# Splitting VectorE's tasks into single instructions, and a planner that ranks by remaining work

## The chip, the core and the metric

The kernel runs on one core of a Trainium2 chip. The metric is the device time of one execution in microseconds (us), the median of several runs. The core has a matrix engine (TensorE; PE in the profile, PEld for its weight loads), a vector engine (VectorE, DVE), a scalar engine (ScalarE, ACT), a general engine (GpSimd, POOL) and queues for transfers (here those of SyncE, SP). Each works through its own list of instructions in the order in which the program issued them; an instruction that needs something of another engine waits, and what is behind it in the list waits too.

## What is computed

Two transformer layers over 16 sequences of 256 tokens with 128 features, all in float32. Each of the four sublayers is added to its input and normalized:

```python
x = L0_attn_hidden_states
x = _layernorm(x + attention0(x))          # 16 heads of 64, softmax over 256 keys
x = _layernorm(x + routed_spline_ffn(x))   # argmax over 8 clusters, then 8 tiles; table lookup
x = _layernorm(x + gated_attention1(x))    # linear attention, and a window of 65 keys, 16 heads of 8
x = _layernorm(x + moe_block(x))           # causal attention, 16 heads of 64, l2-normed q and k;
                                           # then 8 experts 128-512-128
```

The last block is itself two parts: causal attention with a layer norm, and eight experts that all run on all tokens, `gelu(h @ w1[e] + b1[e]) @ w2[e] + b2[e]`, summed with softmax gates and normalized again.

## The kernel before

The 4096 tokens are cut into eight groups of 512 tokens (`NG`, two sequences each), and each group passes five stages: `stage_a` (first attention), `stage_b` (spline feed-forward), `stage_c` (linear and window attention), `stage_d` (causal attention and gates), `stage_e` (the experts). The intermediate results stay on the chip. Buffers are slots of classes (`SLOTS`, lines 39 to 63): five slots for a group's tokens (`x`), five for the experts' hidden values (`hid`), one for their sum (`e`), four PSUM banks (`p`, 512 values of float32 per partition each) and two double banks for scores (`s`).

No loop sets the order of the instructions. Each stage hands tasks to a planner, `Plan.add(eng, cost, fn, r, w, ...)` (line 101): an engine letter (P TensorE, V VectorE, S ScalarE, G GpSimd, Q the queue of transfers; two letters leave the choice to the planner), an estimated cost in ns, a function that issues the instructions, and the objects read and written. An object may be given with a part, `(object, part)`; accesses with different parts don't order each other (line 117). What a task needs but only to hold a slot is given as `hold`. Each task carries a place `at`, which is the group's number plus the stage's offset (`OFF`, 0 to 4) plus a fraction inside the stage.

`Plan.order` (line 144) then simulates all engines. At each step it takes, for each engine, the ready task with the smallest key and among these the smallest again:

```python
key = (start, at, t.seq)
```

`start` is the earliest moment by the planner's own clock: the engine free, each predecessor's end plus a lag (`LAG` by the predecessor's engine, or `OWN` on the same engine), a slot free. A table load of ScalarE adds `SWITCH`, a change of TensorE's tiling mode adds `DRAIN`. So `at` decides only between tasks with equal start. While ScalarE is in a `burst` (the gelus of two experts, eight tasks) it takes nothing else. The instructions are issued in the order of the list that results; the framework adds the waits that the data need. Objects such as `chain_a`, `chain_c`, `chain_d`, `chain_e` are written by the tasks of one kind so that these keep their order.

Tasks of several VectorE instructions in the kernel before: `layernorm` (statistics, line 530; scaling, line 544), `top` in `pair` (line 595: causal mask at L600, two maxima at L605, scaling at L607), `add_up` (L905), `divide` of the linear attention (lines 1002 to 1009), `top` (L1057, L1058) and `divide` (L1102, L1103) of the window attention, `rsqrt` (lines 1145 to 1153, twelve instructions in a row), `keep` (L1199, L1201, on ScalarE or VectorE), `gated` (L1354).

In `stage_e` an expert is four first products into a bank each (line 1337), four gelus (L1339), four tasks `down` (line 1342) that each fill a quarter of one bank `pe_` with four accumulating products (eight matmul instructions), and `gated`, which adds the four quarters with their gates to `moe`:

```python
W.add("P", pe(P, count=NFC), down, r=[we] + hids, w=[(pe_, j)])
...
W.add("V", 4 * 259, gated, r=[pe_, gate], w=[moe])
```

All matmuls pass the helper `mm` (L516), all copies the helper `copy` (L522 on ScalarE, L524 on VectorE).

Of the kernel before, what the change touches and what calls it, by code (L numbers as in the profile page):

```python
# [81 lines left out]


class Plan:

    LAG = {"P": 270.0, "V": 150.0, "S": 170.0, "G": 120.0, "Q": 0.0, "D": 0.0}
    OWN = 80.0
    SWITCH = 1300.0  # L90
    DRAIN = 93.0

    def __init__(self, slots):
# [7 lines left out]
    def add(self, eng, cost, fn, r=(), w=(), at=None, table=None, burst=None, mode="f", hold=()):  # L101
# [137 lines left out]
def kernel(ctx: ExitStack, tc: tile.TileContext, a: dict, out: bass.AP):  # L239
# [286 lines left out]
    def layernorm(o, z, name, after=()):  # L526

        mv, rs = W.buf("m", "mv" + name), W.buf("m", "rs" + name)

        def stats():  # L530
            st = mv()[:, 8 : 8 + NJ * 6].rearrange("p (j s) -> p j s", s=6)
            for j in range(NJ):
                nc.vector.bn_stats(st[:, j, :], z(J, d=D)[:, j, :])  # L533
            for j in range(NJ):
                nc.vector.bn_aggr(mv()[:, 2 * j : 2 * j + 2], st[:, j, :])
# [8 lines left out]
        def scaled():  # L544
            for j in range(NJ):
                nc.vector.tensor_scalar(  # L546
                    o(J, d=D)[:, j, :], z(J, d=D)[:, j, :], mv()[:, 2 * j : 2 * j + 1], rs()[:, j : j + 1],
                    ALU.subtract, ALU.mult,
                )

        W.add("V", NJ * (195 + 70), stats, r=[z, *after], w=[mv])
        W.add("G", 1300, root, r=[mv], w=[rs])
        W.add("V", NJ * 257, scaled, r=[z, mv, rs], w=[o])

# [15 lines left out]
    def pair(pi, qT, kT, v, ov, causal, rq, un=0):  # L570
# [23 lines left out]

        def top():
            s = sps(S2, a=2)
            n = nmx(n=4, pattern="p (a b) -> p a b", a=2)
            if causal:
                diag = s[:, :, P : 3 * P].rearrange("p a (b k) -> p a b k", k=P)
                nc.vector.tensor_tensor(  # L600
                    out=diag, in0=diag, in1=cmask.unsqueeze(1).unsqueeze(1).to_broadcast([P, 2, 2, P]), op=ALU.add
                )
                for qc in range(2):
                    c0, nk = col[qc]
                    nc.vector.tensor_reduce(n[:, :, qc], s[:, :, c0 : c0 + nk], AX.X, ALU.max, negate=True)  # L605
                rqp = rq("p (b i m) -> p i m b", n=16, b=2, i=2)[:, pi, 2 * un : 2 * un + 2, :]
                nc.vector.tensor_tensor(out=n, in0=n, in1=rqp, op=ALU.mult)  # L607
            else:
                nc.vector.tensor_reduce(n, s.rearrange("p a (b k) -> p a b k", k=S), AX.X, ALU.max, negate=True)  # L609

        cost = 1790 if causal else dve(1024)
        W.add("V", cost, top, r=[rq] if causal else [], w=[sps, nmx])

# [206 lines left out]
    def stage_b(g):  # L820
# [81 lines left out]

        def add_up():
            for q, j in enumerate(order):
                V.scalar_tensor_tensor(  # L905
                    y(J, d=D)[:, j, :], pv()[:, q, 65:NPAR], mag()[:, q : q + 1], xx(J, d=D)[:, j, :], ALU.mult, ALU.add
                )

        W.add("V", 4 * 259, add_up, r=[pp, mag, xx], w=[y, end_b])
        W.at = base + 0.95  # L910
# [17 lines left out]
    def stage_c(g):  # L928
# [48 lines left out]
        for b in range(2):  # L977
# [23 lines left out]

            def divide(b=b, pn2=pn2, rden=rden):
                r = rden()[:, :2]
                V.tensor_scalar(r, pn2()[:, :, D], 1e-6, None, ALU.add)
                V.reciprocal(r, r)
                V.tensor_tensor(
                    out=lin(J, d=D)[:, 2 * b : 2 * b + 2, :], in0=pn2()[:, :, :D],
                    in1=r.unsqueeze(2).to_broadcast([P, 2, D]), op=ALU.mult,
                )

            W.add("V", 360 + dve(256), divide, r=[pn], w=[rden, (lin, b)])

            for i, (w0, w1_) in enumerate(win_of):
# [38 lines left out]

                def top(sps=sps, nmx=nmx, nk=nk, t0=t0):
                    s8 = sps("p (u k) -> p u k", u=8)[:, :, :nk]
                    V.tensor_tensor(out=s8, in0=s8, in1=band[:, :, t0 : t0 + nk], op=ALU.add)  # L1057
                    V.tensor_reduce(nmx()[:, :8], s8, AX.X, ALU.max, negate=True)  # L1058

                W.add("V", 130 + 2 * dve(8 * nk), top, w=[sps, nmx])  # L1060
                pts = []
# [38 lines left out]

                def divide(po=po, rw=rw, c0=c0):
                    V.reciprocal(rw()[:, :QC], po()[:, QC : 2 * QC])  # L1102
                    V.tensor_tensor(out=winT()[:, c0 : c0 + QC], in0=po()[:, :QC], in1=rw()[:, :QC], op=ALU.mult)  # L1103

                W.add("V", 700, divide, r=[po], w=[rw, (winT, (b, i))])

# [32 lines left out]
    def rsqrt(o, x, n, eps):  # L1139

        ve, y, u = W.buf("m", "ve"), W.buf("m", "y"), W.buf("m", "u")

        def go():
            V = nc.vector
            V.tensor_scalar(ve(n=n), x(n=n), eps, None, ALU.add)
            yi = y(n=n).bitcast(I32)
            V.tensor_scalar(yi, ve(n=n).bitcast(I32), 1, None, ALU.logical_shift_right)
            V.tensor_scalar(yi, yi, -1.0, float(0x5F3759DF), ALU.mult, ALU.add)
            for k in range(3):
                src, dst = (y, o) if k % 2 == 0 else (o, y)  # L1150
                V.tensor_mul(u(n=n), src(n=n), src(n=n))
                V.scalar_tensor_tensor(u(n=n), u(n=n), -0.5, ve(n=n), ALU.mult, ALU.mult)
                V.scalar_tensor_tensor(dst(n=n), u(n=n), 1.5, src(n=n), ALU.add, ALU.mult)  # L1153

        W.add("V", 2465 + 12 * (n - 16), go, r=[x], w=[ve, y, u, o])

    def stage_d(g):
# [9 lines left out]
        def half(b, hf):  # L1167
# [13 lines left out]
            for u in range(2):  # L1181
# [11 lines left out]

                def keep(e, ps_q=ps_q, qT=qT, u=u):
                    for i in range(2):
                        p = 2 * (2 * hf + u) + i
# [116 lines left out]
    def stage_e(g):  # L1313
# [3 lines left out]
        W.at = base  # L1317
        n = NJ * NE
        tg, gT, pb2, moe = W.buf("p", "tg"), W.buf("k1", "gT"), W.buf("p", "pb2"), W.buf("e", "moe")
        W.add("P", pe(P, passes=1), lambda: nc.tensor.transpose(tg()[:n, :P], gate(n=n), ident), r=[gate], w=[tg], hold=[gT])  # L1320
        W.add("VS", (dve(P), scl(P)), lambda e: copy(e, gT()[:n, :P], tg()[:n, :P]), r=[tg], w=[gT])
        W.add("P", pe(512), lambda: mm(pb2(), gT()[:n, :P], b2blk.rearrange("p j d -> p (j d)")), r=[gT], w=[pb2], hold=[moe])
        W.add("VS", (dve(512), scl(512)), lambda e: copy(e, moe(), pb2()), r=[pb2], w=[moe])
        for e_ in range(NE):
# [10 lines left out]
            for c in range(NFC):  # L1335
                ph, hid = W.buf("p", "phE"), W.buf("hid", "hid")
                W.add("P", pe(512), lambda ph=ph, we=we, c=c: mm(ph(), we()[:, c * P : (c + 1) * P], h2()), r=[we, h2], w=[ph, chain_e], burst=burst, hold=[hid])
# [12 lines left out]

            def gated(e_=e_, pe_=pe_):
                for j in range(NJ):
                    m = moe()[:, j * D : (j + 1) * D]
                    V.scalar_tensor_tensor(m, pe_()[:, j * D : (j + 1) * D], gate()[:, j * NE + e_ : j * NE + e_ + 1], m, ALU.mult, ALU.add)  # L1354

            W.add("V", 4 * 259, gated, r=[pe_, gate], w=[moe])
        W.at = base + 1.0
# [50 lines left out]
```

## Time and profile before

| what | value |
|---|---|
| median of 3 runs | 2237.85 us (2234.47 to 2239.24) |
| the profiled execution | 2238.21 us |
| its span, first to last instruction | 2236.3 us |
| instructions | 49748 |
| mean granted TensorE clock | 0.982 |
| ACT table loads | 59, together 75.7 us |
| transfers | 47.96 MB, mean 21 GB/s |

The profile is of one execution. "Busy" is the time in which an engine has an instruction in work, by the records; the ends of matmuls are modelled. A group row gives the line, the engine, the operation, output<-input by name, the shapes, the number of instructions, then the busy time and the mean length in ns of one, then the idle time of the engine just before them, with what ended it. A timeline row gives start and length in us. The first slice of the span (0 to 55.9 us) has TensorE busy for 38.85 us, the following ones mostly for 51 to 56 of 55.9.

### The profile page before, as it was taken

The numbers are of one execution on the slowest core, as the hardware profiler recorded it, in microseconds if no ns is written. First come the engines' busy times: TensorE is split into PE (matmuls) and PEld (weight loads), VectorE is DVE, ScalarE is ACT, GpSimd is POOL, SyncE is SP. The second block draws the span as 40 slices with busy tenths as digits, with TensorE's granted clock in tenths as the row PEclk, the third lists the DMA queues.
The fourth block names the chain that finished last, engine by engine and source line by source line (L and its number), as shares of the span: only waits on it lengthen the run. The fifth ranks groups of instructions, "written<-read, shape, count | busy, mean of one in ns | idle before, by whom it ended". The sixth has DMA issues, their size and how long they took to land.

```text
span 2236.3 us, 49748 instructions
## 1 busy us (share of the span) xinstructions
PE 2103.2 (94%) x18506; PEld 1566.6 (70%) x18506; DVE 1662.7 (74%) x4784; ACT 1308.2 (58%) x3817; POOL 799.6 (36%) x1443
## 2 busy tenths in 40 slices
PE   6999999999999998999999999999899989989987
PEld 5777877777777765776777777777667667766655
DVE  4788899887588874788767895788866984784742
ACT  3556666665567743676656664666545755654632
POOL 6435363344043531335304360243502530431311
PEclk8999999999999999999999999999999999999988
DMA  6100000000100001000011001100011001101101
GB/s 145 25 1 2 2 1 1 2 2 20 48 21 2 2 24 34 25 6 2 20 39 30 2 1 39 39 6 2 1 43 35 6 1 54 29 1 43 39 20 43
DMA packets 61026, 47.96 MB, mean 21 GB/s; under 512 B 4609, under 2 KB 51297, under 8 KB 60785
## 3 DMA queue, kind: packets, MB, share of 16 engines
q1 hardware_dynamic: 59200, 43.09, 7.0%
q8 instruction: 146, 2.39, 0.4%
q0 software_dynamic: 1008, 0.65, 0.4%
q10 hardware_dynamic: 576, 1.05, 0.2%
q14 instruction: 96, 0.78, 0.1%
HBM read 41.89 MB, written 2.88 MB: 20 GB/s over the span
## 4 chain that ended last, share of the span: by engine, by line
PE 54%; DVE 19%; ACT 5%; issue 2%; POOL 2%; POOLq 0%; DVEq 0%; ACTq 0%
PE p L516 39%; PE s L516 7%; PE p L655 5%; DVE m L605 2%; ACT pb L627 2%; PE p L1075 2%; DVE s L600 1%; DVE m L533 1%; DVE m L609 1%; DVE x L546 1%; POOL pb L640 1%; DVE m L607 1%; PE p L1258 1%; DVE e L1354 1%; DVE uq L1201 1%
## 5 line engine op out<-in xcount | busy, mean ns | idle before, releaser
L640 POOL TENSOR_SCALAR pb<-pb,m 128x256 f32<-128x256 f32 (+1 forms) x1024 | 451.4, 458 | 765.4 <-DVE m L634 671.4
L1339 ACT ACTIVATE hid<-p,b 128x512 f32<-128x512 f32 x256 | 170.4, 688 | 305.6 <-PE p L516 291.4
L655 PE MATMUL p<-ident,pb 128*128 128x128 f32 x1792 | 291.3, 283 | 23.4 <-POOL pb L640 13.9
L627 ACT ACTIVATE pb<-s,m,m 128x128 f32<-128x128 f32 (+1 forms) x512 | 257.3, 522 | 60.2 <-DVE m L607 50.0
L655 PEld LDWEIGHTS p<-ident,pb 128*128 128x128 f32 x1792 | 207.6, 142 | 112.3 <-POOL pb L640 57.1
L627 ACT ACTIVATE pb<-s,m 128x256 f32<-128x256 f32 x512 | 238.7, 489 | 70.1 <-DVE m L609 59.7
L516 PE MATMUL p<-h,we 128*128 128x512 f32 x512 | 265.5, 619 | 9.5 <-ACT hid L1339 4.9
L516 PEld LDWEIGHTS p<-we,hid 128*128 128x128 f32 x2048 | 241.1, 193 | 29.4 <-issue 15.7
L516 PE MATMUL p<-we,hid 128*128 128x128 f32 x2048 | 250.6, 278 | 3.9 <-ACT hid L1339 2.1
L522 ACT COPY pt<-p 128x512 f32<-128x512 f32 (+1 forms) x316 | 168.6, 540 | 144.2 <-PE p L655 132.3
L1354 DVE SCALAR_TENSOR_TENSOR e<-p,m,e 128x128 f32<-128x128 f32 x256 | 71.9, 343 | 143.9 <-PE p L516 122.2
L609 DVE TENSOR_REDUCE m<-s 128x4 f32<-128x1024 f32 x128 | 154.4, 1214 | 27.1 <-PE s L516 26.1
L1248 POOL TENSOR_TENSOR kn<-kn,m 128x512 f32<-128x512 f32 x64 | 66.2, 1049 | 283.4 <-DVE m L1153 231.8
L1069 ACT ACTIVATE pbC<-s,m 128x96 f32<-128x96 f32 (+1 forms) x512 | 135.3, 382 | 33.8 <-DVE m L1058 29.2
L516 PE MATMUL s<-ua,ua 64*128 64x256 f32 x1024 | 141.0, 399 | 10.4 <-ACT pb L627 9.0
L516 PE MATMUL s<-ud,uq 64*128 64x128 f32 (+1 forms) x1024 | 118.9, 355 | 21.3 <-ACT pb L627 20.3
L516 PE MATMUL p<-pt,ua 128*64 128x256 f32 x1024 | 136.7, 390 | 1.3 <-ACT pt L522 0.9
L524 DVE COPY pt<-p 128x512 f32<-128x512 f32 (+1 forms) x196 | 120.7, 620 | 22.0 <-PE p L655 20.3
L605 DVE TENSOR_REDUCE m<-s 128x2 f32<-128x256 f32 (+1 forms) x256 | 130.6, 552 | 5.3
L516 PEld LDWEIGHTS p<-h,we 128*128 128x128 f32 x512 | 85.6, 194 | 64.8 <-issue 31.1
L1024 POOL TENSOR_TENSOR qm<-c,hm 128x512 f32<-128x512 f32 x64 | 68.1, 1069 | 153.9 <-PE s L516 134.2
L516 PEld LDWEIGHTS s<-ua,ua 64*128 64x128 f32 x1024 | 92.0, 188 | 39.8 <-ACT pb L627 14.2
(299 smaller groups left out, 4309.8 us busy)
## 6 DMA issues: line engine op xcount, KB each, us to landing
we<-in_L_ffn_w_dram SPq DMA_DIRECT2D x128, 256.0 KB, 2.7
x<-_attn_hidden_states_dram SPq DMA_DIRECT2D x8, 256.0 KB, 6.7
out_dram<-x SPq DMA_DIRECT2D x8, 256.0 KB, 2.3
dpad<-k SPq DMA_DIRECT2D x1, 768.0 KB, 10.3
wq<-in_L_attn_Wq_dram ACTq DMA_DIRECT2D x2, 256.0 KB, 6.2
wkv<-in_L_attn_Wkv_dram ACTq DMA_DIRECT2D x2, 256.0 KB, 7.1
wkv<-in_L_attn_Wkv_dram SPq DMA_DIRECT2D x2, 256.0 KB, 8.7
wo<-in_L_attn_Wo_dram SPq DMA_DIRECT2D x1, 512.0 KB
```

Of the source, the lines that this page charges most:

```text
L516: nc.tensor.matmul(o, lhsT=lhsT, rhs=rhs, start=start, stop=stop)
L522: nc.scalar.copy(o, i)
L524: nc.vector.tensor_copy(o, i)
L605: nc.vector.tensor_reduce(n[:, :, qc], s[:, :, c0 : c0 + nk], AX.X, ALU.max, negate=True)
L609: nc.vector.tensor_reduce(n, s.rearrange("p a (b k) -> p a b k", k=S), AX.X, ALU.max, negate=True)
L627: act(pb()[:, c0 : c0 + nk], s[:, par, c0 : c0 + nk], AF.Exp, bias=nmx()[:, 2 * par + qc : 2 * par + qc + 1], accum_out=sums()[:, 2 * par ...
L640: eng.tensor_scalar(pb()[:, c0 : c0 + nk], pb()[:, c0 : c0 + nk], sums()[:, 2 * par + qc : 2 * par + qc + 1], 1.0, ALU.mult, ALU.mult,)
L655: nc.tensor.transpose(tps()[:, at * P : (at + 1) * P], pb()[:, c0 + kc * P : c0 + (kc + 1) * P], ident)
L1024: (V if e == "V" else G).tensor_tensor(out=qm("p (h q) -> p h q", q=QC), in0=qw()[:, c0 : c0 + QC].unsqueeze(1).to_broadcast(nq), in1=hm8. ...
L1069: act(pb("p (u k) -> p u k", u=4)[:, u, :nk], s8[:, hp, :nk], AF.Exp, bias=nmx()[:, hp : hp + 1])
L1339: W.add("S", 571, lambda ph=ph, hid=hid, ec=ec: act(hid(), ph(), AF.Gelu_apprx_tanh, bias=b1[:, ec : ec + 1]), r=[ph], w=[hid], table="gel ...
L1354: V.scalar_tensor_tensor(m, pe_()[:, j * D : (j + 1) * D], gate()[:, j * NE + e_ : j * NE + e_ + 1], m, ALU.mult, ALU.add)
```

## The change

It has three parts. The planner: new `LAG` values, an `OWN` for each engine, parts that may be tuples of a kind and a number (different kinds conflict, `overlap`), and before the ordering each task's `at` is lowered by the longest chain of costs and lags that hangs on it, divided by `REST`. The tasks: each of the VectorE tasks named above becomes one task per instruction, with its own cost and, where the instructions differ only in a part of the tile, its own part. The experts: the first products also wait for the object `begun`, written by the copy that sets up `moe`.

```diff
+def overlap(a, b):
+    kind = lambda x: x[0] if isinstance(x, tuple) and isinstance(x[0], str) else type(x)
+    return a is None or b is None or a == b or kind(a) != kind(b)
...
-    LAG = {"P": 270.0, "V": 150.0, "S": 170.0, "G": 120.0, "Q": 0.0, "D": 0.0}
-    OWN = 80.0
+    LAG = {"P": 265.0, "V": 178.0, "S": 200.0, "G": 60.0, "Q": 0.0, "D": 0.0}
+    OWN = {"P": 0.0, "V": 130.0, "S": 80.0, "G": 80.0, "Q": 0.0, "D": 0.0}
+    REST = 30000.0
...
-                    if part is None or q is None or q == part:
+                    if overlap(q, part):
...
     def order(self):
+        rest = {}
+        for t in reversed(self.tasks):
+            rest[t.seq] = min(t.cost) + max([self.LAG[t.eng[0]] + rest[n.seq] for n in t.then], default=0.0)
+            t.at -= rest[t.seq] / self.REST
...
-                        start = max(start, end + (self.OWN if x == e else self.LAG[x]))
+                        start = max(start, end + (self.OWN[x] if x == e else self.LAG[x]))
...
-        W.add("V", NJ * (195 + 70), stats, r=[z, *after], w=[mv])
+        for j in range(NJ):
+            W.add("V", 195, lambda j=j: nc.vector.bn_stats(st(j), z(J, d=D)[:, j, :]), r=[z, *after], w=[(mv, ("j", j))])
+        for j in range(NJ):
+            W.add("V", 70, lambda j=j: nc.vector.bn_aggr(mv()[:, 2 * j : 2 * j + 2], st(j)), w=[(mv, ("j", j))])
...
-        cost = 1790 if causal else dve(1024)
-        W.add("V", cost, top, r=[rq] if causal else [], w=[sps, nmx])
+            W.add("V", 560, ..., w=[sps])                                        # mask
+                W.add("V", 15 + 2 * nk * 1.05, ..., r=[sps], w=[(nmx, qc)])      # two maxima
+            W.add("V", 70, ..., r=[rq], w=[nmx])                                 # scaling
...
-        W.add("V", 4 * 259, add_up, r=[pp, mag, xx], w=[y, end_b])
+            W.add("V", 259, ..., r=[pp, mag, xx], w=[(y, ("j", j)), (end_b, j)])
...
-            W.add("V", 360 + dve(256), divide, r=[pn], w=[rden, (lin, b)])
+            W.add("V", 70, ..., r=[pn], w=[rden])
+            W.add("V", 70, ..., w=[rden])
+            W.add("V", dve(256), ..., r=[pn, rden], w=[(lin, b)])
...
-                W.add("V", 130 + 2 * dve(8 * nk), top, w=[sps, nmx])
+                W.add("V", 15 + 1.05 * 8 * nk, ..., w=[sps])
+                W.add("V", 15 + 1.05 * 8 * nk, ..., r=[sps], w=[nmx])
...
-                W.add("V", 700, divide, r=[po], w=[rw, (winT, (b, i))])
+                W.add("V", 420, ..., r=[po], w=[rw])
+                W.add("V", 130, ..., r=[po, rw], w=[(winT, (b, i))])
...
-        W.add("V", 2465 + 12 * (n - 16), go, r=[x], w=[ve, y, u, o])
+        each = lambda fn, r, w: W.add("V", 60 + n, fn, r=r, w=w)                 # twelve times
...
-                W.add("VS", (782, 714), keep, r=[ps_q], w=[qT])
+                    W.add("VS", (391, 357), keep, r=[ps_q], w=[(qT, i)])         # for i in 0, 1
...
-        W.add("VS", (dve(512), scl(512)), lambda e: copy(e, moe(), pb2()), r=[pb2], w=[moe])
+        W.add("VS", (dve(512), scl(512)), lambda e: copy(e, moe(), pb2()), r=[pb2], w=[moe, begun])
...
-                W.add("P", pe(512), ..., r=[we, h2], w=[ph, chain_e], burst=burst, hold=[hid])
+                W.add("P", pe(512), ..., r=[we, h2, begun], w=[ph, chain_e], burst=burst, hold=[hid])
...
-            W.add("V", 4 * 259, gated, r=[pe_, gate], w=[moe])
+                W.add("V", 259, gated, r=[(pe_, j), gate], w=[(moe, ("j", j))])  # for j in 0 to 3
```

In the diff "..." also stands for the function of a task where it issues the same instruction as before. The split of the layer norm's scaling (one task of 257 for each quarter) is like that of its statistics.

More of the change, by code (lines that the diff above doesn't have):

```diff
@@ L528, in layernorm @@
         mv, rs = W.buf("m", "mv" + name), W.buf("m", "rs" + name)
[L530 to L535, printed above, removed]
+        st = lambda j: mv()[:, 8 + 6 * j : 14 + 6 * j]
+        for j in range(NJ):
+            W.add("V", 195, lambda j=j: nc.vector.bn_stats(st(j), z(J, d=D)[:, j, :]), r=[z, *after], w=[(mv, ("j", j))])
+        for j in range(NJ):
+            W.add("V", 70, lambda j=j: nc.vector.bn_aggr(mv()[:, 2 * j : 2 * j + 2], st(j)), w=[(mv, ("j", j))])
         def root():
@@ L542, in root @@
             nc.gpsimd.tensor_tensor(out=rs()[:, 0:NJ], in0=rs()[:, NJ : 2 * NJ], in1=mhalf, op=ALU.pow)
-        def scaled():
-            for j in range(NJ):
-                nc.vector.tensor_scalar(
+        W.add("G", 1300, root, r=[mv], w=[rs])
+        for j in range(NJ):
+            W.add(
+                "V", 257,
+                lambda j=j: nc.vector.tensor_scalar(
                     o(J, d=D)[:, j, :], z(J, d=D)[:, j, :], mv()[:, 2 * j : 2 * j + 1], rs()[:, j : j + 1],
                     ALU.subtract, ALU.mult,
-                )
-        W.add("V", NJ * (195 + 70), stats, r=[z, *after], w=[mv])
-        W.add("G", 1300, root, r=[mv], w=[rs])
-        W.add("V", NJ * 257, scaled, r=[z, mv, rs], w=[o])
+                ),
+                r=[z, mv, rs] if o is not z else [mv, rs], w=[(o, ("j", j))],
+            )
     def transposed(o, z, name, scale=None, shift=None, after=()):
@@ L593, in pair @@
         W.add("P", pe(ncol, cols=0), scores, r=[qT, kT], w=[sps, chain[0]], mode="r")
[L595 to L601, printed above, removed]
-                )
[L603 to L609, printed above, removed]
@@ L611, in pair @@
-        cost = 1790 if causal else dve(1024)
-        W.add("V", cost, top, r=[rq] if causal else [], w=[sps, nmx])
+        nm = lambda: nmx(n=4, pattern="p (a b) -> p a b", a=2)
+        if causal:
+            diag = lambda: sps(S2, a=2)[:, :, P : 3 * P].rearrange("p a (b k) -> p a b k", k=P)
+            W.add(
+                "V", 560,
+                lambda: nc.vector.tensor_tensor(
+                    out=diag(), in0=diag(), in1=cmask.unsqueeze(1).unsqueeze(1).to_broadcast([P, 2, 2, P]), op=ALU.add
+                ),
+                w=[sps],
+            )
+            for qc in range(2):
+                c0, nk = col[qc]
+                W.add(
+                    "V", 15 + 2 * nk * 1.05,
+                    lambda qc=qc, c0=c0, nk=nk: nc.vector.tensor_reduce(
+                        nm()[:, :, qc], sps(S2, a=2)[:, :, c0 : c0 + nk], AX.X, ALU.max, negate=True
+                    ),
+                    r=[sps], w=[(nmx, qc)],
+                )
+            rqp = lambda: rq("p (b i m) -> p i m b", n=16, b=2, i=2)[:, pi, 2 * un : 2 * un + 2, :]
+            W.add("V", 70, lambda: nc.vector.tensor_tensor(out=nm(), in0=nm(), in1=rqp(), op=ALU.mult), r=[rq], w=[nmx])
+        else:
+            W.add(
+                "V", dve(1024),
+                lambda: nc.vector.tensor_reduce(
+                    nm(), sps(S2, a=2).rearrange("p a (b k) -> p a b k", k=S), AX.X, ALU.max, negate=True
+                ),
+                r=[sps], w=[nmx],
+            )
@@ L901, in stage_b @@
         y = W.buf("b", "yB")
-        def add_up():
-            for q, j in enumerate(order):
-                V.scalar_tensor_tensor(
+        for q, j in enumerate(order):
+            W.add(
+                "V", 259,
+                lambda q=q, j=j: V.scalar_tensor_tensor(
                     y(J, d=D)[:, j, :], pv()[:, q, 65:NPAR], mag()[:, q : q + 1], xx(J, d=D)[:, j, :], ALU.mult, ALU.add
-                )
-        W.add("V", 4 * 259, add_up, r=[pp, mag, xx], w=[y, end_b])
+                ),
+                r=[pp, mag, xx], w=[(y, ("j", j)), (end_b, j)],
+            )
         W.at = base + 0.95
@@ L1000, in stage_c @@
             pn2 = lambda pn=pn: pn("p (i n) -> p i n", i=2)
[L1002 to L1006, printed above, removed]
+            rd = lambda rden=rden: rden()[:, :2]
+            W.add("V", 70, lambda pn2=pn2, rd=rd: V.tensor_scalar(rd(), pn2()[:, :, D], 1e-6, None, ALU.add), r=[pn], w=[rden])
+            W.add("V", 70, lambda rd=rd: V.reciprocal(rd(), rd()), w=[rden])
+            W.add(
+                "V", dve(256),
+                lambda b=b, pn2=pn2, rd=rd: V.tensor_tensor(
                     out=lin(J, d=D)[:, 2 * b : 2 * b + 2, :], in0=pn2()[:, :, :D],
-                    in1=r.unsqueeze(2).to_broadcast([P, 2, D]), op=ALU.mult,
-                )
-            W.add("V", 360 + dve(256), divide, r=[pn], w=[rden, (lin, b)])
+                    in1=rd().unsqueeze(2).to_broadcast([P, 2, D]), op=ALU.mult,
+                ),
+                r=[pn, rden], w=[(lin, b)],
+            )
             for i, (w0, w1_) in enumerate(win_of):
@@ L1053, in stage_c @@
                 nmx = W.buf("m", "nmxC")
[L1055 to L1058, printed above, removed]
-                W.add("V", 130 + 2 * dve(8 * nk), top, w=[sps, nmx])
+                s8 = lambda sps=sps, nk=nk: sps("p (u k) -> p u k", u=8)[:, :, :nk]
+                W.add(
+                    "V", 15 + 1.05 * 8 * nk,
+                    lambda s8=s8, nk=nk, t0=t0: V.tensor_tensor(out=s8(), in0=s8(), in1=band[:, :, t0 : t0 + nk], op=ALU.add),
+                    w=[sps],
+                )
+                W.add(
+                    "V", 15 + 1.05 * 8 * nk,
+                    lambda s8=s8, nmx=nmx: V.tensor_reduce(nmx()[:, :8], s8(), AX.X, ALU.max, negate=True), r=[sps], w=[nmx],
+                )
                 pts = []
@@ L1099, in stage_c @@
                 rw = W.buf("m", "rw")
-                def divide(po=po, rw=rw, c0=c0):
-                    V.reciprocal(rw()[:, :QC], po()[:, QC : 2 * QC])
-                    V.tensor_tensor(out=winT()[:, c0 : c0 + QC], in0=po()[:, :QC], in1=rw()[:, :QC], op=ALU.mult)
-                W.add("V", 700, divide, r=[po], w=[rw, (winT, (b, i))])
+                W.add("V", 420, lambda po=po, rw=rw: V.reciprocal(rw()[:, :QC], po()[:, QC : 2 * QC]), r=[po], w=[rw])
+                W.add(
+                    "V", 130,
+                    lambda po=po, rw=rw, c0=c0: V.tensor_tensor(out=winT()[:, c0 : c0 + QC], in0=po()[:, :QC], in1=rw()[:, :QC], op=ALU.mult),
+                    r=[po, rw], w=[(winT, (b, i))],
+                )
         W.at = base + 0.95
@@ L1141, in rsqrt @@
         ve, y, u = W.buf("m", "ve"), W.buf("m", "y"), W.buf("m", "u")
[L1143 to L1153, printed above, removed]
-        W.add("V", 2465 + 12 * (n - 16), go, r=[x], w=[ve, y, u, o])
+        V = nc.vector
+        yi = lambda: y(n=n).bitcast(I32)
+        each = lambda fn, r, w: W.add("V", 60 + n, fn, r=r, w=w)
+        each(lambda: V.tensor_scalar(ve(n=n), x(n=n), eps, None, ALU.add), [x], [ve])
+        each(lambda: V.tensor_scalar(yi(), ve(n=n).bitcast(I32), 1, None, ALU.logical_shift_right), [ve], [y])
+        each(lambda: V.tensor_scalar(yi(), yi(), -1.0, float(0x5F3759DF), ALU.mult, ALU.add), [], [y])
+        for k in range(3):
+            src, dst = (y, o) if k % 2 == 0 else (o, y)
+            each(lambda src=src: V.tensor_mul(u(n=n), src(n=n), src(n=n)), [src], [u])
+            each(lambda: V.scalar_tensor_tensor(u(n=n), u(n=n), -0.5, ve(n=n), ALU.mult, ALU.mult), [ve], [u])
+            each(lambda src=src, dst=dst: V.scalar_tensor_tensor(dst(n=n), u(n=n), 1.5, src(n=n), ALU.add, ALU.mult), [u, src], [dst])
     def stage_d(g):
@@ L1192, in half, with keep @@
                 W.add("S", scl(512), lambda sq_q=sq_q, ps_q=ps_q: act(sq_q(), ps_q(), AF.Square), r=[ps_q], w=[sq_q])
-                def keep(e, ps_q=ps_q, qT=qT, u=u):
-                    for i in range(2):
+                for i in range(2):
+                    def keep(e, ps_q=ps_q, qT=qT, u=u, i=i):
                         p = 2 * (2 * hf + u) + i
@@ L1318, in stage_e @@
         n = NJ * NE
+        begun = object()
         tg, gT, pb2, moe = W.buf("p", "tg"), W.buf("k1", "gT"), W.buf("p", "pb2"), W.buf("e", "moe")
@@ L1336, in stage_e @@
                 ph, hid = W.buf("p", "phE"), W.buf("hid", "hid")
-                W.add("P", pe(512), lambda ph=ph, we=we, c=c: mm(ph(), we()[:, c * P : (c + 1) * P], h2()), r=[we, h2], w=[ph, chain_e], burst=burst, hold=[hid])
+                W.add("P", pe(512), lambda ph=ph, we=we, c=c: mm(ph(), we()[:, c * P : (c + 1) * P], h2()), r=[we, h2, begun], w=[ph, chain_e], burst=burst, hold=[hid])
                 ec = e_ * NFC + c
@@ L1349, in stage_e, with gated @@
                 W.add("P", pe(P, count=NFC), down, r=[we] + hids, w=[(pe_, j)])
-            def gated(e_=e_, pe_=pe_):
-                for j in range(NJ):
+            for j in range(NJ):
+                def gated(e_=e_, pe_=pe_, j=j):
                     m = moe()[:, j * D : (j + 1) * D]
                     V.scalar_tensor_tensor(m, pe_()[:, j * D : (j + 1) * D], gate()[:, j * NE + e_ : j * NE + e_ + 1], m, ALU.mult, ALU.add)
-            W.add("V", 4 * 259, gated, r=[pe_, gate], w=[moe])
+                W.add("V", 259, gated, r=[(pe_, j), gate], w=[(moe, ("j", j))])
         W.at = base + 1.0
```

## The prediction

> **What bounds the kernel now.** First the page's busy times, to see which engine can set the time at all; then busy times by stretch, because five stages overlap; then the groups of VectorE; last single instructions in order of time, for what a wait costs.
>
> ```profile
> PE 2103.2 (94%) x18506; PEld 1566.6 (70%) x18506; DVE 1662.7 (74%) x4784; ACT 1308.2 (58%) x3817; POOL 799.6 (36%) x1443
> ...
> PE 54%; DVE 19%; ACT 5%; issue 2%; POOL 2%; POOLq 0%; DVEq 0%; ACTq 0%
> ```
>
> TensorE looks full at 94%, and that is too kind. A 128x512 matmul is shown as 619 ns and a 128x128 one as 278 ns (group means), but in an unbroken run the next starts after 0.43 and 0.11 us; 128x256 ones after 0.216 us, half-height or half-width pairs after 0.21 (256 columns) or 0.10 us a pair. Counts times these: 656 x 0.43 + 1600 x 0.216 + 6500 x 0.11 + 3072 x 0.105 + 2112 x 0.051 + 4600 narrow ones x 0.015 = 1844 us. So about 390 of the 2236 us are not matmul streaming. Some of it a new order can't take: 5 us before the first matmul, 9 us at 21 us into the span (POOL sets up constants), 15 us after the last matmul, and some 840 changes between tilings of the array, each with about 0.1 to 0.15 us of empty array, near 100 us. Roughly 250 us is left, in holes mostly under 0.2 us. That is the most that could be won.
>
> ```profile
> 1184.00:1341.00 157.00, 152.47 (x1451) 114.19 (x1450) 136.65 (x392) 110.47 (x359) 82.89 (x149) 1.00 0.03 8
> 1341.00:1428.00 87.00, 85.68 (x555) 61.47 (x558) 50.01 (x164) 40.55 (x72) 6.61 (x10) 1.00 0.15 43
> 1716.00:1835.00 119.00, 107.00 (x1204) 82.00 (x1193) 107.86 (x348) 74.14 (x224) 56.13 (x88) 0.97 0.03 8
> ```
>
> Columns: stretch, length, busy PE, weight loads, DVE, ACT, POOL, clock, DMA. Work alternates: about 170 us in which the attentions run and DVE is 85 to 91% busy, then about 90 us in which the experts of one group run and DVE is half idle. TensorE is the bound in the second kind; in the first it shares the bound with DVE.
>
> ```profile
> L600 DVE TENSOR_TENSOR s<-s,cmask 128x512 f32<-128x512 f32 x128 | 88.4, 691 | 22.1 <-PE s L516 21.6
> L605 DVE TENSOR_REDUCE m<-s 128x2 f32<-128x512 f32 x128 | 86.9, 679 | 0.0
> L1354 DVE SCALAR_TENSOR_TENSOR e<-p,m,e 128x128 f32<-128x128 f32 x256 | 71.9, 343 | 143.9 <-PE p L516 122.2 <-issue 21.7
> ...
> 1012.03 0.19 DVE L1151 TENSOR_TENSOR m<-m 128x32 f32<-128x32 f32 x1
> 1012.26 0.19 DVE L1152 SCALAR_TENSOR_TENSOR m<-m,m 128x32 f32<-128x32 f32 x1
> 1012.49 0.19 DVE L1153 SCALAR_TENSOR_TENSOR m<-m,m 128x32 f32<-128x32 f32 x1
> ...
> 2216.40 4.11 PE L516 MATMUL p<-we,hid 128*128 128x128 f32 x32
> ...
> 2220.55 1.12 DVE L1354 SCALAR_TENSOR_TENSOR e<-p,m,e 128x128 f32<-128x128 f32 x4 [5.34 <-PE p L516]
> 2221.59 0.86 DVE L533 BATCH_NORM_STATS2 m<-e 128x6 f32<-128x128 f32 x4
> ```
>
> Two things to see. The three small instructions each need the one before: they start 0.228 us apart, 0.035 us after the end of the last. The four statistics need nothing of each other: (0.86 - 0.277)/3 = 0.194 us apart, 0.083 us before the end. So a dependent neighbour costs VectorE 0.035 + 0.083 = 0.118 us. And L1354's first instruction reads only the first quarter of the bank that 32 matmuls fill; that quarter was complete after the first eight of them, near 2217.5, yet it starts at 2220.55, after the last. In all 64 experts it starts no earlier than 38 ns after the thirty-second matmul. The wait is by bank, not by quarter.
>
> **What the skill says.** Perfetto Trace Analysis (Identifying the Most-Contended Engine) calls matmul busy time a bad measure because matmuls are pipelined; 2103 against 1844 us agrees. Its Optimizing Scalar/DVE Operations says that where VectorE isn't saturated but makes bubbles elsewhere, breaking up its work may let it finish sooner: the idea of this edit; no run shows it yet. TensorEngine Tiling (Key Properties) says that a change of tiling mode drains the array; the trace agrees, with the 0.1 to 0.15 us above. PSUM — Partial Sum Buffer (PSUM bank collisions raise a hardware error) says that TensorE writing a bank while VectorE reads the same one is an error, so a program must keep the two apart; the 64 waits above are that.
>
> **The change, part by part.** No instruction is added or dropped; only the order on each engine changes, and which of ACT and DVE takes a copy. The sum is made against the profiled execution: span 2236.3, with 1.9 us around it 2238.2, 0.02% over the median shown.
>
> 1. Dependent steps taken apart. Inside the tasks that are split there are, in a row on VectorE: mask, maximum, scaling in the causal softmax, 2 x 128; addition and maximum in the window softmax, 64; reciprocal and product there, 64; the inverse root, 11 x 32 = 352; the linear attention's division, 2 x 16 = 32. Sum 768; by 0.118 = 91 us of VectorE, 11 us a group. Other work can be put there now. In the expert stretches VectorE is idle anyway, so it brings nothing; in the attention stretches (two thirds of the time, and all these steps lie there) I take that TensorE gains half of what VectorE gains, as each is near 90%: 45 us. Bounds: 0 (a chain's own latency is unchanged, and if TensorE waits for the chain and not for the queue, nothing is won) and 91.
>
> 2. The planner's constants. New LAG for V is 178, which is the 83 ns that an end lies after the next start plus the 94 ns (median) from a DVE end to a POOL start; G 60 against 54 ns from a POOL end to a PE start; OWN of P 0, as matmuls run back to back; OWN of V 130 against 118. All are nearer to the trace than 150, 120, 80, 80. Only the new costs of single VectorE tasks are short: 560, 284 and 553 where the trace has about 607, 340 and 597. A truer plan has fewer waits in the queues: 10 us, from 0 to 20.
>
> 3. Longest work first. It decides only between tasks that can start at the same planned moment, so on a loaded TensorE queue. The rest of a score task runs through chain_e, 32 x (860 + 265) = 36 us a group, or 1.2 of the planner's units beside the unit of the group itself; worked through for the five stages their offsets become about 0.85 group instead of 1, much the old order. But the experts' second products lead only to the last layer norm (rest some 15 us) and come last of all, though they free five hidden buffers, a bank and in the end a slot of x. I book nothing here, bounds -25 and +40. At the end, 2124 to 2157 (24 of 33 us PE busy), more filler may be left: 5 us won.
>
> 4. L1354 by quarters. Now each instruction is ordered after its own quarter: product 0, product 1, quarter 0, product 2, quarter 1, product 3. By the wait for the whole bank quarter 0 stands until product 1 is done, and product 2, behind it in the order, must stand until quarter 0 has been read: 0.167 us from the last matmul's start interval to its end (0.278 - 0.111), 0.04 to VectorE, 0.343 for the instruction, 0.055 back: 0.6 us of TensorE, and the same before product 3. Everything behind on TensorE's in-order queue waits too, then ACT for its next products. In 41 of 64 experts the 32 matmuls now run with nothing between: 41 x 2 x 0.6 = 49 us lost. In the other 23 a foreign matmul group covers it. Bounds: 8 (the last group alone, 8 x 2 x 0.6 less what another first product covers) and 64 x 1.2 = 77. The trace of before never has the read order inside the writes, so the way back (product waits for quarter) is inferred from the bank rule.
>
> 5. The rest (layer norms, L905, division, halves of the scaled queries): all before or after on the same engine; the last layer norms are a serial 15 us and keep it. The last quarters save 0.5 us. At nothing.
>
> Sum: -45 - 10 - 5 + 49 = -11, and the planner's free choice of orders, which it makes for its own model: I put -10, from the holes of 250 us. 2238 - 21 = 2217 us.
>
> **Rivals.** A. Forecast: gains and bank waits both real, 2217, own range 2190 to 2245; chance 0.40. B. The bank waits stay covered by other matmuls, since low priority spreads the products: 2238 - 60 = 2178; chance 0.20. For it: 23 experts are already spread; against: the expert stretches have little else. C. Slower: the bank. Products come last, so nothing is left to stand between them: all 64 pay 1.2 us, 77 us, and the bank and hidden buffers are held as long, while VectorE's saved time falls where TensorE waits for chains (gain 20): 2238 + 57 = 2295. It decides as soon as more than about 50 experts run unbroken with reads in between; chance 0.35. For it: 41 do already, and VectorE is 19% of the chain against TensorE's 54%. D. The planner interleaves nothing that counts, VectorE's time was slack: 2238, chance 0.05.
>
> **Numbers.** 0.2%, about 4.5 us, is what a measurement can tell. Faster: 0.7 of A, all but a little of B: 0.28 + 0.2 = 0.48. Slower: 0.2 of A, nearly all of C, some of D: 0.08 + 0.34 + 0.01 = 0.43. Same: 0.09. Range 2160 to 2310, which leaves the outer ends of B and C out.
>
> **What would show it.** Step 1: DVE's busy sum falls by 40 us or more at equal counts, the inverse root's instructions no longer stand 0.228 us apart. Step 4: L1354 in pieces of one, and second products with idle time before them released by DVE e L1354, near 0.6 us; in the last 60 us the period of an expert goes from 7.4 to 8.6 us. If those waits are absent the bank reading is wrong and B holds; if TensorE's waits for ACT pb and POOL pb grow instead, it is step 3.

## The result: slower by 2.3%

| | median us | runs |
|---|---|---|
| before | 2237.26 | 2234.47 to 2239.24 |
| after | 2289.26 | 2285.61 to 2290.07 |

The ratio is 1.023, with a 95% interval of 1.0212 to 1.0248: 52 us lost, where 21 us less were forecast. The profiled execution of after has a span of 2283.7 us, 47.4 more than before.

First the page of after, in the order in which before was read: busy times, the chain that ended last, and two of the costliest groups.

```profile
PE 2124.5 (93%) x18506; PEld 1589.7 (70%) x18506; DVE 1662.4 (73%) x4911; ACT 1259.7 (55%) x3692; POOL 794.5 (35%) x1443
...
PE 61%; DVE 23%; issue 6%; ACT 6%; POOL 3%; SPq 1%; DMA 1%; POOLq 0%; DVEq 0%; ACTq 0%
...
L530 PE MATMUL p<-we,hid 128*128 128x128 f32 x2048 | 276.7, 283 | 41.6 <-DVE e L1386 39.3
...
L538 DVE COPY pt<-p 128x512 f32<-128x512 f32 (+1 forms) x316 | 190.7, 620 | 32.0 <-PE p L679 28.8
```

The same two groups in before:

```profile
L516 PE MATMUL p<-we,hid 128*128 128x128 f32 x2048 | 250.6, 278 | 3.9 <-ACT hid L1339 2.1
...
L524 DVE COPY pt<-p 128x512 f32<-128x512 f32 (+1 forms) x196 | 120.7, 620 | 22.0 <-PE p L655 20.3
```

The matrix work is the same 18506 instructions, yet TensorE now shows idle time before the experts' second products (`p<-we,hid`): 41.6 us, of which `DVE e L1386` ended 39.3. Before, it was 3.9 us. L1386 is the old L1354, the quarter sum. VectorE's busy sum has not fallen at all, 1662.4 against 1662.7, and it has 127 instructions more, ACT 125 fewer: copies have moved. Of the copies named `pt` VectorE does 316 now, 196 before.

The stretches of two groups in after; columns as in the same view of before (stretch, length, busy PE, weight loads, DVE, ACT, POOL, clock, DMA).

```profile
1215.00:1391.00 176.00, 170.39 (x1605) 131.06 (x1606) 156.85 (x473) 110.33 (x365) 86.48 (x154) 1.00 0.03 8
1391.00:1475.00 84.00, 78.03 (x663) 56.97 (x655) 45.64 (x127) 43.16 (x94) 9.86 (x19) 1.00 0.15 39
```

The alternation has stayed. In the stretch of the attentions VectorE is busy for 89% (85 to 91% before). In the stretch of the experts TensorE is busy for 93%, in the next one of this kind for 95%, where three such stretches of before had 99, 98 and 93%. That is a hint and no more, as the borders of the stretches are drawn by hand. What the loss consists of can be seen in single instructions, here the timeline of after near its end (start, length in us, the instructions merged; weight loads left out).

```profile
2210.77 1.50 PE L530 MATMUL p<-we,hid 128*128 128x128 f32 x12
...
2212.38 0.35 DVE L1386 SCALAR_TENSOR_TENSOR e<-p,m,e 128x128 f32<-128x128 f32 x1 [8.13 <-PE p L530]
...
2212.78 1.16 PE L530 MATMUL p<-we,hid 128*128 128x128 f32 x8 [0.51 <-DVE e L1386]
...
2213.98 0.35 DVE L1386 SCALAR_TENSOR_TENSOR e<-p,m,e 128x128 f32<-128x128 f32 x1 [1.25 <-PE p L530]
...
2214.38 1.16 PE L530 MATMUL p<-we,hid 128*128 128x128 f32 x8 [0.44 <-DVE e L1386]
...
2215.58 0.61 DVE L1386 SCALAR_TENSOR_TENSOR e<-p,m,e 128x128 f32<-128x128 f32 x2 [1.25 <-PE p L530]
```

Products 0 and 1 end, quarter 0 is summed, product 2 starts when it has been; product 2 ends, quarter 1 is summed, product 3 starts. TensorE and VectorE take turns on one bank. Each turn shows as an idle time of about 0.45 us before the matmul, and takes 0.6 us or a little more of streaming, since the end of the last matmul before it (0.278 us long, 0.111 from start to start) is also waited out. A border is the step from the last matmul of one second product to the first of the next, from start to start, where both belong to one expert and no other matmul stands between. Of these borders 68 are longer than 0.3 us, with 43.3 us in all beyond the usual 0.111; in before there is none. Counted over all of TensorE's steps, also those with another matmul between, `DVE e L1386` ends 92 that are more than 0.15 us longer than usual, 54.7 us in all (before: 7, 5.1 us).

### The profile page after: what moved, and what is told of

Read it like the earlier page. It is cut to its first block, busy times and chain, and to the rows that moved or that the text cites. A ratio compares the mean times of both kernels' runs of the same rounds, so it can differ in the third digit from the quotient of the medians.

```text
span 2283.7 us, 49853 instructions
## 1 busy us (share of the span) xinstructions
PE 2124.5 (93%) x18506; PEld 1589.7 (70%) x18506; DVE 1662.4 (73%) x4911; ACT 1259.7 (55%) x3692; POOL 794.5 (35%) x1443
## 4 chain that ended last, share of the span: by engine, by line
PE 61%; DVE 23%; issue 6%; ACT 6%; POOL 3%; SPq 1%; DMA 1%; POOLq 0%; DVEq 0%; ACTq 0%
PE p L530 44%; PE s L530 7%; PE p L679 6%; ACT pb L651 2%; DVE m L632 2%; POOL pb L664 2%; DVE s L1084 2%; PE p L1105 2%; DVE m L622 2%; DVE e L1386 2%; DVE pt L538 1%; DVE m L1089 1%; DVE s L613 1%; DVE m L1263 1%; DVE x L561 1%
## 5 line engine op out<-in xcount | busy, mean ns | idle before, releaser
L530 PE MATMUL p<-we,hid 128*128 128x128 f32 x2048 | 276.7, 283 | 41.6 <-DVE e L1386 39.3
L530 PEld LDWEIGHTS p<-we,hid 128*128 128x128 f32 x2048 | 249.6, 193 | 87.7 <-DVE e L1386 66.7
L679 PE MATMUL p<-ident,pb 128*128 128x128 f32 x1792 | 268.0, 282 | 31.0 <-POOL pb L664 21.3
L679 PEld LDWEIGHTS p<-ident,pb 128*128 128x128 f32 x1792 | 201.8, 142 | 104.2 <-POOL pb L664 56.5
L530 PE MATMUL p<-h,we 128*128 128x512 f32 x512 | 258.6, 628 | 6.4 <-ACT hid L1370 4.7
L1386 DVE SCALAR_TENSOR_TENSOR e<-p,m,e 128x128 f32<-128x128 f32 x256 | 84.5, 347 | 234.7 <-PE p L530 230.2
L538 DVE COPY pt<-p 128x512 f32<-128x512 f32 (+1 forms) x316 | 190.7, 620 | 32.0 <-PE p L679 28.8
L536 ACT COPY pt<-p 128x384 f32<-128x384 f32 (+1 forms) x196 | 100.3, 534 | 91.8 <-PE p L679 82.1
L622 DVE TENSOR_REDUCE m<-s 128x2 f32<-128x512 f32 (+1 forms) x256 | 132.2, 549 | 1.0
L530 PE MATMUL p<-pt,ud 128*64 128x256 f32 (+1 forms) x1024 | 112.7, 338 | 2.5 <-ACT ua L752 1.4
```

The source lines that it names most:

```text
L530: nc.tensor.matmul(o, lhsT=lhsT, rhs=rhs, start=start, stop=stop)
L536: nc.scalar.copy(o, i)
L538: nc.vector.tensor_copy(o, i)
L622: lambda qc=qc, c0=c0, nk=nk: nc.vector.tensor_reduce(nm()[:, :, qc], sps(S2, a=2)[:, :, c0 : c0 + nk], AX.X, ALU.max, negate=True),
L679: nc.tensor.transpose(tps()[:, at * P : (at + 1) * P], pb()[:, c0 + kc * P : c0 + (kc + 1) * P], ident)
```

## The experiments

All runs below share their runs of before, whose median was 2238.3 to 2238.8 us.

### The same plan with the quarters held back (e1_quarters_last)

```diff
...
+    def late_quarters(line):
+        done, held = {}, {}
+        for item in line:
+            t = item[0]
+            if id(t) in quarter and done.get(quarter[id(t)], 0) < NJ:
+                held.setdefault(quarter[id(t)], []).append(item)
+                continue
+            yield item
+            if id(t) in product:
+                ...
+                if done[x] == NJ:
+                    yield from held.pop(x, [])
...
-        for t, e, _, _ in line:
+        for t, e, _, _ in late_quarters(line):
```

The plan is made with everything in the change; only the quarter sums are held back when the list is issued. TensorE, ACT and POOL keep their order instruction by instruction. `product` and `quarter` hold the tasks of the second products and of the quarter sums.

> The kernel after with its own plan and the same order of TensorE; only the four quarter sums of an expert (L1386) are held back in the list until the fourth second product has been issued. Bank theory: the 92 stalls of TensorE that DVE e L1386 ends (54.7 us in the trace) go, VectorE's queue moves a little; 2289 falls to 2235 to 2250. Order theory (the ranking by remaining work and the new lags cost the time, the stalls only fill time that would be lost anyway): 2275 or more.

Measured: 2241.4 us, ratio 1.0016 (1.0009 to 1.0022). The view of the quarter sum's line in e1, which here is L1388: who waited for it.

```profile
PEld p L530: 16.1, 31
PE p L530: 5.7, 11
```

In after the same two rows read 67.1 us in 107 times and 39.3 us in 85. No border between products is longer than 0.3 us any more. So 48 of the 52 us go with this one edit: the waits on the shared bank are the cause. Whether they are kept by the bank or by the tile `pe_` can't be told apart here, as the tile fills the bank. With them gone the rest of the change, new order included, is 3 us slower than before, not faster.

### The same waits put into the kernel before (e2_quarters_between, e7_quarters_between)

A quarter sum is issued right behind the product that follows its own; `gated(js=(j,))` adds one quarter.

```diff
...
+            for k, j in ((-4, 0), (-3, 1)):
+                between[id(W.tasks[k])] = (e_, j, started, early, gated)
...
+            issued.add(id(t))
+            if id(t) in between:
+                e_, j, started, early, gated = between[id(t)]
+                if id(started) in issued:
+                    early.add((e_, j))
+                    gated(js=(j,))
```

> The kernel before with its plan and the same order of TensorE; quarter 0 of an expert's sum is issued right after second product 1, quarter 1 after product 2, the other two where all four stood. Bank theory: each unbroken expert (41 of 64) pays twice 0.6 us, the broken ones less: 2238 rises by 40 to 80 us, and DVE e L1354 is the releaser of some 80 to 128 stalls of TensorE. Order theory: within 10 us of before.

In e2 the condition `started` was missing: there the first quarters of some experts are added before the copy that sets up the group's sum, which then overwrites them, so a part of the experts' sum is lost; the amount of work is the same. Measured: 2329.38 us. With the condition:

> As e2_quarters_between, but a quarter is issued early only if the copy that sets up the group's sum has been issued before; else it stays where all four stood. Bank theory: up to 41 unbroken experts pay twice 0.6 us: 2238 plus 40 to 80 us, with DVE e as the releaser of 80 to 128 stalls. Order theory: within 10 us of before.

Measured: 2327.09 us, ratio 1.0402 (1.0384 to 1.042), 88 us slower and a little above the range that was expected. The waits of TensorE in e7, longest in total first (waiting line, what it waited for, us in total, times, longest):

```profile
PE p L516 <- DVE e L1357: 63.8, 117, 2.4
PE s L516 <- ACT pb L627: 29.5, 27, 4.3
PE p L655 <- POOL pb L640: 14.4, 10, 9.7
```

The order of TensorE's work is that of before, and the next waits stay near what they were (ACT pb 30.3, POOL pb 13.9 before); the row on top had 3.9 us in 5 waits. There are 111 borders of over 0.3 us with 77.7 us of excess, 0.70 us each. The same mechanism, switched off in after and switched on in before, takes away 48 us and adds 88.

### The planner told of the whole bank (e3_whole_bank)

```diff
-                W.add("V", 259, gated, r=[(pe_, j), gate], w=[(moe, ("j", j))])
+                W.add("V", 259, gated, r=[pe_, gate], w=[(moe, ("j", j))])
```

> The kernel after, but each quarter sum is told to the planner as reading all of the bank (r=[pe_, gate]), so the whole plan is made anew. Bank theory: no stall by L1386, and the other gains of the change can show: 2215 to 2245. Order theory: 2270 or more.

Measured: 2242.12 us, ratio 1.0013 (1.0004 to 1.0021). The plan is new, the result that of e1. One expression in the change, `(pe_, j)`, carries its loss; without it the change is worth nothing.

### Ranking, lags and splits apart (e4_rest_only, e5_rest_and_lags, e6_rest_and_splits, e8_chains_whole)

e4 is before with these lines and the wait for `begun`; e5 adds the new `LAG` and `OWN`; e6 is e3 with the old `LAG` and `OWN`; e8 is e3 with `top` in `pair` and `rsqrt` as whole tasks again.

```diff
     def order(self):
+        rest = {}
+        for t in reversed(self.tasks):
+            rest[t.seq] = min(t.cost) + max([self.LAG[t.eng[0]] + rest[n.seq] for n in t.then], default=0.0)
+            t.at -= rest[t.seq] / 30000.0
```

> The kernel before with the ranking by remaining work and the wait for begun alone; tasks, lags and costs as before. Bank theory: ranking alone is worth little, within 20 us of 2238. Order theory: most of the 51 us are lost here already, 2270 or more.

> The kernel before with the ranking by remaining work, begun, and the new LAG and OWN values; VectorE's tasks stay whole. The change without the early bank reads measured 2242, the ranking alone 2214, so splits or lags lose about 28 us. Split theory (a split chain takes longer from its first to its last instruction, and ACT and POOL wait for its end): 2205 to 2222. Lag theory (the new values lose it): 2235 or more.

> The kernel after with quarter sums that read all of the bank and with the old LAG and OWN values, so ranking and splits without the new lags. Split theory: 2235 to 2255, mask start to scaling end of a causal pair near 2.8 us as in the kernel after. Lag theory: 2205 to 2222.

> The kernel after with quarter sums that read all of the bank, and with the softmax top of both attentions that use pair and the inverse root as whole tasks again; all other splits, the new lags and the ranking stay. Split theory, with the loss in these two chains: 2205 to 2225, mask start to scaling end back near 2.0 us. Lag theory: 2235 or more, as without this edit.

| run | ranking | lags | splits | us | ratio, interval |
|---|---|---|---|---|---|
| before | | | | 2238 | |
| e4 | yes | | | 2214.09 | 0.9887 (0.987 to 0.9903) |
| e5 | yes | new | | 2230.0 | 0.9967 (0.9953 to 0.998) |
| e6 | yes | | yes | 2234.24 | 0.998 (0.9973 to 0.9987) |
| e3 | yes | new | yes | 2242.12 | 1.0013 (1.0004 to 1.0021) |
| e8 | yes | new | all but two kinds | 2243.67 | 1.0026 (1.0016 to 1.0036) |

The ranking (with the wait for `begun`, which was not run apart) is 24 us faster than before, somewhat more than was expected, and faster than either kernel of this study. On top of it the lags lose 16 us and the splits 20. The 2230 of e5 lies between the ranges of the two theories, and the 2234 of e6 just below that of the split theory, so neither of them holds alone.

A part of this shows in the traces as a lower clock. TensorE's granted clock is full or half at any one time; here is its mean in e4 and in e6:

```profile
core 0: 2212.4 us, clock 0.983
...
core 0: 2233.2 us, clock 0.976
```

TensorE runs at half clock for 76 us in the trace of e4 and for 107 us in that of e6. There a transposition of 128x128 (`p<-ident,pb`) starts 0.214 us after the last one, elsewhere 0.109. Priced at the full-clock steps of the same matmuls, 24 us of streaming fall into these stretches in e4 and 41 us in e6. They take twice as long there, so by this estimate up to 17 of the 21 us between the two traces come with the clock; for the lags, e5 against e4, it is up to 4 of 16. For e1 against before it is up to 13 us (27 and 40 us of streaming), so the rest of the change may hold a gain that the clock takes back. Each half-clock stretch of e4 and of e6 follows 3.4 us in which TensorE was busy for 65% or less, but other such pauses bring none; what sets these stretches off is not shown.

The splits do what they say: neighbours on VectorE that stand 25 to 45 ns apart, the mark of a dependent step, are 1001 in before, 299 in after, 426 in e6. What becomes of one causal pair is in the timeline of VectorE in after:

```profile
1030.29 0.69 DVE L613 TENSOR_TENSOR s<-s,cmask 128x512 f32<-128x512 f32 x1
1030.89 0.17 DVE L548 BATCH_NORM_AGGREGATE m<-m 128x2 f32<-128x6 f32 x1
1030.98 0.39 DVE L538 COPY ov<-p 128x256 f32<-128x256 f32 x1
1031.28 0.68 DVE L622 TENSOR_REDUCE m<-s 128x2 f32<-128x512 f32 x1
1031.88 0.16 DVE L658 RECIPROCAL m<-m 128x2 f32<-128x2 f32 x1
1031.95 0.41 DVE L622 TENSOR_REDUCE m<-s 128x2 f32<-128x256 f32 x1
1032.27 0.55 DVE L538 COPY pt<-p 128x384 f32<-128x384 f32 x1
1032.74 0.16 DVE L658 RECIPROCAL m<-m 128x2 f32<-128x2 f32 x1
1032.81 0.22 DVE L628 TENSOR_TENSOR m<-m,m 128x4 f32<-128x4 f32 x1
```

There is no gap left between mask (L613), maxima (L622) and scaling (L628), but five foreign instructions. VectorE is better filled and the pair is later: from the start of the mask to the end of the scaling it takes 1.95 us in before (median of 128) and 2.79 in after; the inverse root, twelve steps in a row, goes from 2.65 to 5.92 us (median of 32). That this delay costs the time was the split theory, and e8 speaks against it: with both chains whole again (1.95 and 2.65 us) it is no faster, 2243.67.

### Copies kept off VectorE (e13_splits_copies_back, e14_ranking_copies_back)

```diff
+                    if e == "V" and len(t.eng) > 1:
+                        start += 20.0
                     at = t.at
```

In e13 this is added to e6, in e14 to e4.

> e6_rest_and_splits (2234) with a handicap of 20 ns on VectorE for every task that ACT could also take, which decides ties for ACT. Copies theory (the freed time was spent on copies moved to VectorE): VectorE's busy sum falls by 60 us or more and the time to 2225 or less. Slack theory (TensorE did not wait for VectorE's throughput): VectorE's busy sum falls, the time stays at 2228 or more.

> The control: e4_rest_only (2214) with the same handicap of 20 ns. Slack theory: within 12 us of 2214 or slower, though VectorE has less to do. Copies theory: VectorE's queue is what counts, so 2205 or less.

The busy times from the pages of e6 and then e13:

```profile
PE 2097.4 (94%) x18506; PEld 1583.2 (71%) x18506; DVE 1678.8 (75%) x4956; ACT 1242.4 (56%) x3646; POOL 796.3 (36%) x1443
...
PE 2099.2 (93%) x18506; PEld 1583.8 (71%) x18506; DVE 1539.8 (69%) x4667; ACT 1348.5 (60%) x3923; POOL 792.4 (35%) x1443
```

VectorE has 139 us less to do than in e6, of which ACT takes 106; the time rises to 2247.72 us (1.0042, 1.0028 to 1.0056). In e14 it has 62 us less than in e4 (1656.8), and the time rises to 2262.85 (1.0113, 1.0098 to 1.0128). So a smaller load on VectorE was not worth anything here. As ACT got more at the same time, and the order is another one, this does not show that VectorE's throughput never counts; it speaks against the copies as what made the splits worthless.

### What chance in the order is worth (e9, e10, e11, e12)

```diff
-    SWITCH = 1300.0
+    SWITCH = 1320.0
```

This is e9 on before, e10 on e4 and e12 on e3. e11 is e4 with 20000 in place of 30000.

> The kernel before with SWITCH 1320 in place of 1300 and nothing else: a change that should be worth nothing in itself, but gives the planner another order from the first table load on. It measures what chance in the order is worth. If differences of 10 to 15 us between the variants mean something: within 6 us of 2238. If they are chance: off by 10 us or more.

> The ranking alone (2214 as e4_rest_only) with SWITCH 1320. Ranking is a real gain: 2204 to 2224. The 24 us were a lucky order: 2228 or more.

> The ranking alone with remaining work divided by 20000 in place of 30000, so that it weighs more. Ranking is a real gain: 2200 to 2228, again below 2238. Lucky order: on either side of 2238.

> e3_whole_bank (2242) with SWITCH 1320. If the 28 us between it and the ranking alone belong to splits and lags: 2230 to 2252. If they are chance: 2225 or less, or 2260 or more.

Measured: e9 2241.06 us (1.0014, 1.0008 to 1.0021), e10 2215.97 (0.9897, 0.988 to 0.9913), e12 2244.54 (1.0024, 1.0013 to 1.0035). A planner constant that means little moves the time by 2 to 3 us, and the 28 us between e4 and e3 stay with it (e10 and e12). But e11 measured 2238.66 (1.0003, 0.9995 to 1.0011): the ranking's 24 us are there with one weight and gone with another. So the gain hangs on the weight; it is not shown that ranking is a gain in itself.

## Why the prediction was wrong, step by step

The forecast was 2217 us; slower was held possible at 0.43, and the measured time lies 6 us below the 2295 of rival C. A gain was forecast and a loss came. The closeness to C's number is luck: C wanted 77 us from waits in all 64 experts and a gain of 20.

**Step 4, the bank: right in the mechanism, and nearly right in size.** The prediction put 41 x 2 x 0.6 = 49 us. Holding the quarters back takes 48 us out. That they agree to 1 us is partly luck, as the parts differ: 27 unbroken experts instead of 41 and 68 long borders instead of 82, 0.64 us each instead of 0.6, or 43 us, plus waits behind foreign matmuls. That the products come last and wholly unbroken, as C had it, did not happen: fewer experts run unbroken than before. The way back, product waits for quarter, which was inferred there, is in the timeline. One detail was wrong: in the last 60 us the period of an expert was to go from 7.4 to 8.6 us; only the first expert of that stretch takes turns twice, the later ones are summed two quarters at a time, with another expert's first products between.

**Step 1, the dependent steps: the failing step.** The gaps are gone nearly as counted, about 700 of 768; at 0.118 us each that is an estimate of 83 us of VectorE. The term "half of what VectorE gains", -45 us, is what failed. It assumed that TensorE shares its bound with VectorE in the attention stretches since both are near 90% busy. But the planner filled the freed time with some 120 copies from ACT, so VectorE's busy sum did not change by 1 us, and runs in which VectorE has 62 and 139 us less to do were slower. No gain came of this step: the splits on top of the ranking lost 20 us (e6 against e4), up to 17 of them at the lower clock, for which the prediction had no term. The Trainium skill's Perfetto Trace Analysis (Optimizing Scalar/DVE Operations), which the prediction names for the idea of the edit, speaks of breaking up instructions; here only tasks were broken up, so no run tests it.

**Step 2, the constants: wrong sign.** Lags nearer to the trace were to bring 10 us; on top of the ranking they cost 16 (e5 against e4), on top of ranking and splits 8 (e3 against e6).

**Step 3, ranking and the end.** Booked at nothing within -25 and +40: alone it brought 24 us, with a slightly other weight nothing. The 5 us at the end and the 10 us booked for the planner's freedom did not come; what is left of the whole change without the bank waits is 3 us slower.

The sum in its own terms: -45 - 10 - 5 - 10 + 49 = -21 was forecast; measured are about +3 for the first four together and +48 for the last. The largest failing term is VectorE's freed time, -45; the other three didn't come either.

Still open is why lags and splits lose what the ranking wins, beyond the part that comes with the clock, and why the clock is lower there. Each variant is one order out of very many.

## What to carry to other kernels

When a task that reads the result of several others is cut so that it starts after the first of them, ask what unit is really kept apart: here it was a whole bank with its tile, so reading a finished quarter early stopped the writer of the next. In this case a dependency that the planner did not know (2289 us) was worse than one that it knew too broadly (2242). And high busy shares on two engines do not say that relieving one speeds the other: try a load taken off before counting it. When variants of an order are compared, compare the granted clock too.

## What the runs showed of the hardware

A bank that is written and read in turn cost TensorE 0.64 us (after) to 0.70 us (e7) a turn for a VectorE instruction of 0.35 us; the rest is the end of the last matmul and two hand-overs. In before an independent neighbour starts on VectorE 0.083 us before the end of the one ahead and a dependent one 0.035 us after it, and the change removed 700 such gaps without the kernel becoming faster, which was not expected. The mean granted clock, 0.975 in after and 0.982 in before, is made of full clock and of stretches at half clock, 116 and 80 us in all.
